# Two expert stages re-ordered into 36 block-and-chunk steps, with chunk-wise sums in PSUM and the weight products moved inside

## The chip, the cores and the metric
The program runs on one core of a Trainium2 chip. A core has a matrix engine (TensorE, PE in the profile, with PEld for its weight loads), a vector engine (VectorE, DVE), a scalar engine (ScalarE, ACT), GpSimd (POOL) and SyncE (SP), which here issues nearly all DMA transfers. Each engine has its own list of instructions and waits for the others by semaphores. The metric is the device time of one execution in microseconds (us), lower is better.

## The reference
A two-layer network in float32 on tokens `x` of 4 x 512 with 128 features. Each half layer normalises the tokens and adds its result to them. The order that the kernel follows is: an expert stage (half weight), linear attention, a second expert stage (half weight, the same weights), then the second layer's product-key feed-forward part and softmax attention, and the feed-forward part once more.

The expert stage matters here. Per token, 16 gate scores pass through a sigmoid; the two best of four groups and the four best experts in them are chosen, and their weights are normalised:

```
scores = sigmoid(x @ w_gate.T)
...
w = w / (w.sum(-1) + 1e-6)
out = sum_e w[e] * (silu(x @ w1[e].T) * (x @ w3[e].T)) @ w2[e].T  +  shared expert
```

Linear attention, which follows, uses random features: `phi(t) = relu(t @ RF)` for queries and keys, `kv = phi_k^T v`, and `out = phi_q kv / (phi_q sum(phi_k)) @ W_out`. Since RF and W_out act on fixed weights, products of weights with weights (W_qk with RF, W_v with W_out, and W_q with the keys of the feed-forward part) can be formed before any token is needed.

## The kernel before
**The stages.** `net` (L1505) runs `moe` (first expert stage), `linear_fold` and `peer_fold` (products of weights), `linear_attn`, `moe` again, `peer_and_scores`, `attn` and `peer`.

**An expert stage.** The 2,048 tokens are four blocks of 512. All 16 experts of 64 hidden features lie side by side as eight chunks of 128 columns; the shared expert of 128 is a ninth chunk, index `NCH` = 8, which needs no gate weight. `hidden` (L335) makes one chunk for a block of tokens: two matrix products of 128x512 (`pg` L342, `pu` L344), a silu on ACT (L346) and a product on DVE (L350, or L348 for the ninth chunk). `weigh` (L353) multiplies a chunk by the spread gate weights on POOL (L355). `out` (L357) makes the result of 128 tokens: nine accumulated products in one PSUM tile `po` (L360), and DVE adds half of it to the tokens (`residual`, L175). So `out` of the first 128 tokens needs all nine weighted chunks of the block.

**The gate.** `stats` and `normed` normalise a block (DVE, with two small POOL operations L111 and L113), `scores` (L227) turns it on PE (L230), copies it on ACT (L232), and makes the gate logits (L238) and the sigmoid (L242). Then come four pieces on DVE, the chain: `pairs` (L244, seven operations), `groups` (L277, nine), `best` (L289) and `choose` (L304), whose last operation writes the weights `w` (L318). `weights` (L332) turns `w` on PE (`pcT` L324), copies it on ACT (`cT` L326), writes it to memory with one DMA (L165), and reads it back with two DMAs of 1 MB (L170), spread over the partitions.

**The order.** Inside `moe` the order of PE, DVE, ACT and POOL is that of the Python program (`manual_schedule`, L202). The first block makes its nine chunks while the gates of blocks 0 and 1 are worked out; all of its multiplications on POOL stand behind it (L420). From the second block on, the outputs of the block before are made between the last four chunks (L408), each chunk is weighed one step later (L417), and the last block's outputs stand at the end (L425). Products `pg` and `pu` take turns in five PSUM tiles (`m_ps`, L199). Outside `moe` a scheduler orders the instructions.

**Other work in the first expert stage.** Behind block 0 stands `distances` (L992: small operations on DVE and ACT, and 22 small DMAs), behind block 1 the loads for linear attention (`linear_loads`, four DMAs, 2.25 MB), behind block 2 the loads for the second layer (`peer_weights` and `attn_weights`, 22 DMAs on SP). Loads are issued by SP in this order, between the DMAs of the gate weights. `linear_fold` (L441) and `peer_fold` (L630) are then 112 passes of PE over 64 rows each, all passes of one half of the rows before those of the other half, each group copied out by ACT or DVE. At the start, the token loads alternate between SP's and ACT's queues (L80).

Of the kernel before, what the change touches and what calls it, by code (L numbers as in the profile page):

```python
# [10 lines left out]
FP = mybir.dt.float32  # L11
AF = mybir.ActivationFunctionType
# [5 lines left out]
P = 128  # L18
# [44 lines left out]
class Net:  # L63
# [12 lines left out]
    def tokens(self, lo, hi):  # L76
        x_tok = self.t["x"].flatten_outer_dims()
        for i in range(lo, hi):
            xi = self.const.tile([P, DIM], FP, tag=f"x{i}", name=f"x{i}")
            eng = self.nc.sync if i % 2 else self.nc.scalar  # L80
            eng.dma_start(xi, x_tok[i * P : (i + 1) * P, :])
            self.xs.append(xi)
# [110 lines left out]
    def moe(self, behind=None, ahead=None):  # L193

        nc, tc = self.nc, self.tc
        with (
# [123 lines left out]
            def given(w):  # L320

                pc = ps1.tile([NE, SEQ], FP, tag="gate", name="pcT")
                for i in range(BT):
                    nc.tensor.transpose(pc[:, i * P : (i + 1) * P], w[:, i, :], self.ident)  # L324
                cT = sb.tile([NE, SEQ], FP, tag="cT", name="cT")
                nc.scalar.copy(cT, pc)  # L326
                return self.spread(sb, sd, [(cT, slice(0, NE))])

            class Experts(Gate):


                def weights(u):  # L332
                    u.cw = given(u.w)

                def hidden(u, *cs):  # L335
                    if not hasattr(u, "hT"):
                        u.hT = sb.tile([P, NCH + 1, SEQ], FP, tag="hT", name="hT")
                        u.hs = {}
                    for c in cs:
                        cols = slice(c * P, (c + 1) * P)  # L340
                        pg = ps.tile([P, SEQ], FP, tag="mm", name="pg")
                        nc.tensor.matmul(pg, self.w1[:, cols], u.xT, start=True, stop=True)  # L342
                        pu = ps.tile([P, SEQ], FP, tag="mm", name="pu")
                        nc.tensor.matmul(pu, self.w3[:, cols], u.xT, start=True, stop=True)  # L344
                        g = sb.tile([P, SEQ], FP, tag="g", name="g", bufs=NCH + 1)
                        nc.scalar.activation(g, pg, AF.Silu)  # L346
                        if c == NCH:
                            nc.vector.tensor_tensor(u.hT[:, c, :], pu, g, ALU.mult)  # L348
                        else:
                            nc.vector.tensor_tensor(g, pu, g, ALU.mult)  # L350
                            u.hs[c] = g

                def weigh(u, *cs):  # L353
                    for c in cs:
                        nc.gpsimd.tensor_tensor(u.hT[:, c, :], u.hs[c], u.cw[:, c, :], ALU.mult)  # L355

                def out(u, i):  # L357
                    po = pso.tile([P, DIM], FP, tag="po", name="po")
                    for c in range(NCH + 1):
                        nc.tensor.matmul(  # L360
                            po,
                            u.hT[:, c, i * P : (i + 1) * P],
                            self.w2[:, c, :],
                            start=(c == 0),
                            stop=(c == NCH),
                        )
                    self.residual(u.blk * BT + i, po, 0.5)

            def chain(u):
                return [u.pairs, u.groups, u.best, u.choose]

            behind = behind or {}
            blocks = [Experts(blk) for blk in range(NB)]
            if ahead:
# [8 lines left out]
            for blk in range(NB):  # L385
                now, last = blocks[blk], blocks[blk - 1] if blk else None
                after = blocks[blk + 1] if blk + 1 < NB else None
                parts = []
                now.hidden(NCH)
                if last is None:  # L390
                    parts = chain(now)
                elif after:
                    after.scores()
                    parts = chain(after)
                for c in range(NCH):
                    if parts:
                        parts.pop(0)()
                    now.hidden(c)
                    if last is None:
                        if c == 3:  # L400
                            after.scores()
                            parts = chain(after)
                        if c == 4:
                            now.weights()
                        if c in (5, 6):
                            blocks[c - 3].stats()
                    else:
                        if c >= NCH - BT:  # L408
                            last.out(c - NCH + BT)
                        if after and c == 4:  # L410
                            after.weights()
                        if ahead and (blk, c) in ahead:
                            ahead[blk, c](ps)
                    if c == 7 and blk + 2 < NB:
                        blocks[blk + 2].normed()
                    if last and c:
                        now.weigh(c - 1)  # L417
                if last is None:
                    after.weights()
                    now.weigh(*range(NCH))  # L420
                else:
                    now.weigh(NCH - 1)
                for f in behind.get(blk, []):
                    f()
            for i in range(BT):  # L425
                now.out(i)
# [14 lines left out]
    def linear_fold(self, pool):  # L441


        nc, tc = self.nc, self.tc
        self.wf = wf = pool.tile([P, 2, H * DH], FP, tag="wf", name="wf")
        self.wvo = wvo = pool.tile([P, NHP, 2, DIM], FP, tag="wvo", name="wvo")
        self.bout = self.load(pool, "bout", [P, DIM], self.t["b_out"].partition_broadcast(P))
        self.tiny = pool.tile([P, 1], FP, tag="tiny", name="tiny")
        nc.vector.memset(self.tiny, 1e-6)
        with tc.tile_pool(name="af_ps", bufs=4, space=PSUM, reuse_waits="tile") as ps:  # L450
            for s in range(2):
                for odd in range(2):
                    r = slice(odd * DH, (odd + 1) * DH)
                    pf = ps.tile([P, NHP, DH], FP, tag="pf", name="pf")
                    for k in range(NHP):
                        nc.tensor.matmul(
                            pf[:, k, :],
                            self.wqkT[r, s * NHP + k, :],
                            self.rf[r, k, :],
                            start=True,  # L460
                            stop=True,
                        )
# [1163 lines left out]
```

## Time and profile before

| what | us | from |
|---|---|---|
| median of three runs | 1448.12 | times |
| lowest and highest | 1443.87, 1449.14 | times |
| profiled execution, first to last instruction | 1447.6 | the page |
| first expert stage, to the last `po` | 0 to 130.6 | timeline of PE |
| products of weights | 130.6 to 149.4 | timeline of PE |
| linear attention | 149.4 to 310.1 | timeline of PE |
| second expert stage | 310.1 to 426.8 | timeline of PE |
| the rest | 426.8 to 1447.6 | timeline of PE |

Of the profiled execution only the span is given; its own device time is not listed apart from the three runs, whose median lies 0.5 us above the span. In the two expert stages PE was busy 111.1 of 130.6 us and 106.6 of 116.7 us, POOL 49.2 and 45.1 us. A row of the timeline gives the start, the length of a run of equal instructions, the engine, the line, and in brackets how long the engine sat idle before and what ended that. One matrix product in float32 is two passes of PE, so `x2` is one product of 512 columns; at full clock such products follow each other every 0.86 us, though one is listed with 1.02 us because its end overlaps the next. Lengths near 1.9 us for the same thing are passes at half clock.

### The profile page before, as it was taken

How to read it: one execution, taken by the hardware profiler on the slowest of the kernel's cores; microseconds unless marked ns; L12 is line 12 of the kernel's file. 1: busy time of each engine (PE TensorE's matmuls, PEld its weight loads, DVE VectorE, ACT ScalarE, POOL GpSimd, SP SyncE). 2: the span in 40 equal slices, each digit the busy share in tenths (PEclk: the TensorE clock that was granted, in tenths of full speed). 3: DMA queues.
4: the chain of work that ended last, by engine and by line, in shares of the span. 5: the costliest groups of instructions: out<-in, count | busy, mean ns of one | idle time of the engine just before them, and what ended most of it. 6: DMA issues, size and time to landing. Idle time of an engine off the chain costs nothing.

```text
span 1447.6 us, 32427 instructions
## 1 busy us (share of the span) xinstructions
PE 1211.2 (84%) x12424; PEld 772.2 (53%) x12424; DVE 917.5 (63%) x2583; ACT 846.0 (58%) x1621; POOL 754.3 (52%) x760
## 2 busy tenths in 40 slices
PE   6899989987995789798887589899899889777776
PEld 3559566654662555555564145465464555544455
DVE  5642422257529887977953166666676677598997
ACT  4331323332227577676644488978778778487774
POOL 1532333215347978888967014435344443478874
PEclk9898899998997799999988789999999999988888
DMA  3583041215500035343449878978889874000000
GB/s 107 112 195 112 1 103 42 59 35 130 106 1 1 29 103 189 117 163 142 175 183 285 305 214 233 278 204 244 256 223 274 234 208 126 8 2 6 6 8 10
DMA packets 180805, 189.23 MB, mean 131 GB/s; under 512 B 44091, under 2 KB 155307, under 8 KB 180523
## 3 DMA queue, kind: packets, MB, share of 16 engines
q1 hardware_dynamic: 177930, 185.51, 44.5%
q8 instruction: 98, 1.61, 0.5%
q10 hardware_dynamic: 2592, 1.64, 0.4%
q14 instruction: 57, 0.46, 0.1%
q0 software_dynamic: 128, 0.01, 0.0%
HBM read 135.13 MB, written 52.13 MB: 129 GB/s over the span
## 4 chain that ended last, share of the span: by engine, by line
PE 44%; DVE 19%; ACT 16%; POOL 8%; DMA 6%; issue 4%; SPq 1%; ACTq 0%; DVEq 0%; POOLq 0%
ACT F L1325 6%; DVE wt L822 5%; PE po L360 4%; PE pg L342 4%; PE pu L344 4%; PE pq L1128 4%; DVE rep L783 3%; ACT ht L1290 3%; PE po L1409 3%; PE p L1088 3%; PE ph L1277 3%; POOL al L758 2%; DMA F<-S 2%; PE pk L503 2%; PE pu L525 2%
## 5 line engine op out<-in xcount | busy, mean ns | idle before, releaser
L1265 POOL TENSOR_TENSOR F<-F,kz 128x512 f32<-128x512 f32 (+10 forms) x88 | 164.5, 1872 | 263.4 <-DMA F<-S 183.4
L758 POOL TENSOR_TENSOR al<-sim 128x512 f32<-128x512 f32 x128 | 138.6, 1114 | 42.9 <-ACT sim L717 39.4
L1310 DVE CUSTOM_DVE_ANT_0 F<-pf,F 128x64 f32<-128x64 f32 (+21 forms) x256 | 99.4, 437 | 84.3 <-PE pf L1299 42.6
L1290 ACT ACTIVATE ht<-ph,b 128x2048 f32<-128x2048 f32 (+7 forms) x65 | 102.2, 1572 | 84.6 <-PE ph L1277 84.5
L1325 ACT ACTIVATE F<-F,mn 128x64 f32<-128x64 f32 (+21 forms) x256 | 129.7, 508 | 0.3
L1142 ACT ACTIVATE st<-pq 128x256 f32<-128x256 f32 (+3 forms) x128 | 82.8, 698 | 71.1 <-PE pq L1128 37.8
L355 POOL TENSOR_TENSOR hT<-g,spread 128x512 f32<-128x512 f32 x64 | 79.7, 1268 | 79.0 <-DVE g L350 51.5
L1128 PE MATMUL pq<-k,q 32*128 32x256 f32 (+3 forms) x1024 | 102.5, 493 | 12.0 <-POOL q L1105 9.0
L828 POOL TENSOR_TENSOR wt<-wt 128x1152 f32<-128x1152 f32 x32 | 84.1, 2627 | 48.7 <-DVE wt L822 44.7
L1356 DVE COPY wT<-pt 128x512 f32<-128x512 f32 (+1 forms) x176 | 104.4, 635 | 7.0 <-PE pt L1350 4.8
L815 ACT ACTIVATE wt<-al,z 128x576 f32<-128x576 f32 x128 | 88.8, 768 | 29.4 <-DVE z L808 20.0
L346 ACT ACTIVATE g<-pg 128x512 f32<-128x512 f32 x72 | 42.7, 597 | 103.3 <-PE pg L342 96.6
L783 DVE MATCH_REPLACE8 rep<-top,al 128x576 f32<-128x576 f32 x128 | 95.1, 743 | 0.0
L1299 PE MATMUL pf<-ht,w2b 64*32 64x512 f32 (+16 forms) x1408 | 86.8, 538 | 8.2 <-ACT ht L1290 8.2
L1350 PE MATMUL pt<-ident,F 128*128 128x128 f32 x640 | 91.1, 285 | 0.5 <-issue 0.5
L884 PE MATMUL po<-up,cT 128*128 128x128 f32 x256 | 45.5, 332 | 53.8 <-DVE cT L880 53.8
L822 DVE SCALAR_TENSOR_TENSOR wt<-rep,wt 128x2304 f32<-128x2304 f32 x32 | 88.5, 2764 | 0.0
L1409 PEld LDWEIGHTS po<-wT,v 128*64 128x64 f32 x2560 | 76.9, 138 | 20.3 <-DVE wT L1356 9.4
L1350 PEld LDWEIGHTS pt<-ident,F 128*128 128x128 f32 x640 | 72.3, 145 | 27.8 <-issue 14.7
L1409 PE MATMUL po<-wT,v 128*64 128x64 f32 x2560 | 80.6, 223 | 4.0 <-DVE wT L1356 2.1
L1098 DVE TENSOR_TENSOR t<-p,cos 128x512 f32<-128x512 f32 x64 | 43.8, 685 | 59.4 <-POOL k L1106 28.1
L344 PE MATMUL pu<-ln_xT,w 128*128 128x512 f32 x144 | 78.3, 627 | 2.6 <-DVE g L350 2.6
(218 smaller groups left out, 2833.3 us busy)
## 6 DMA issues: line engine op xcount, KB each, us to landing
spread<-rows SPq DMA_DIRECT2D x24, 1024.0 KB
S<-st SPq DMA_DIRECT2D x32, 512.0 KB
S<-st SPq DMA_DIRECT2D x32, 384.0 KB
V<-v SPq DMA_DIRECT2D x16, 512.0 KB
S<-st SPq DMA_DIRECT2D x32, 256.0 KB
v<-V SPq DMA_DIRECT2D x16, 512.0 KB
F<-S SPq DMA_DIRECT2D x24, 256.0 KB
S<-st SPq DMA_DIRECT2D x32, 128.0 KB
```

The lines of the kernel that those rows point to most:

```text
L344: nc.tensor.matmul(pu, self.w3[:, cols], u.xT, start=True, stop=True)
L758: nc.gpsimd.tensor_tensor(u.al[:, h, :NEAR].rearrange("p (i j) -> p i j", j=NK), bc(u.sim[:, 0, h, :TK], 2, NK), bc(u.sim[:, 1, h], 1, TK) ...
L783: nc.vector.match_replace(u.rep[:, h, :], u.top[:, h, :], u.al[:, h, :ALL], LOWEST)
L822: nc.vector.scalar_tensor_tensor(wf, u.rep.rearrange("p h k -> p (h k)"), TAKEN, wf, ALU.is_lt, ALU.mult)
L1128: nc.tensor.matmul(pq[hh // 2][:, hh % 2, :J], u.q[r, t, a, :], u.k[r, t, a, :J], start=(a == 0), stop=(a == 1), tile_position=(hh * 32, 0),)
L1265: nc.gpsimd.tensor_tensor(u.F[:, :, :J], u.F[:, :, :J], win, ALU.add)
L1290: nc.scalar.activation(ht, x, AF.Gelu, bias=self.b1)
L1310: nc.vector.tensor_tensor_reduce(F, pf[k % 2][:, k // 2, :J], F, -1.0, -LOWEST, ALU.add, ALU.min, mn[:, g : g + 1],)
L1325: nc.scalar.activation(F, F, AF.Exp, bias=mn[:, g : g + 1], scale=-1.0, accum_out=sm[:, g : g + 1],)
L1350: nc.tensor.transpose(pt[:, at : at + P], u.F[:, m - 1 - s0 - s, j * P : (j + 1) * P], self.ident,)
L1356: nc.vector.tensor_copy(u.unit.wT[:, js.start : js.stop, :, q : q + w * GQ].rearrange("p j h (r q) -> p j h r q", q=2), pt[:, : len(js) * ...
L1409: nc.tensor.matmul(po[o * DH : (o + 1) * DH, c, :], vs[u.t.n - u.t.ib + j][:, h * DH : (h + 1) * DH], u.wT[:, j, h, x : x + nq], start=(j ...
```

## The change
A stage becomes one row of 36 steps, a step being a block and a chunk, the ninth chunk of each block first. In step k, `hidden` makes chunk k. From step 10 on, up to two chunks are weighed per step, at most up to chunk k-2, and up to two chunks go into the output. `out` now adds one chunk to all four token tiles of the block, in one PSUM tile of 128x4x128, and only the last chunk's turn is followed by four `residual`s. The weighted chunks `hT` are single tiles, five in all; the unweighted ones, `g`, have fourteen. The gates of the later blocks are worked out at fixed steps. The spread weights come back in eight DMAs of 256 KB per block instead of two of 1 MB.

In the first stage the other work becomes hooks at fixed steps: the loads for linear attention at step 17, `distances` at 20, the loads of the second layer at 22, and the products of weights at steps 29 to 32 and 35, with the two halves of the rows alternating. `linear_fold` and `peer_fold` as stages of their own are gone. An activation table that serves both exp and ln is loaded once in `distances`. All token loads but the first four go through SP's queue.

```diff
-            eng = self.nc.sync if i % 2 else self.nc.scalar
+            eng = self.nc.sync if i % 2 or i >= BT else self.nc.scalar
...
+                    for c in range(0, NCH, 2):
+                        w = sb.tile([P, 2, SEQ], FP, tag="spread", name="spread", bufs=NCH)
+                        for o in range(2):
+                            at = d[2 * c + o : 2 * c + 4 : 2, :]
+                            at = bass.AP(at.tensor, at.offset, [[0, DH], *at.ap])
+                            nc.sync.dma_start(w[o * DH : (o + 1) * DH], at)
+                        u.cw += [w[:, 0, :], w[:, 1, :]]
...
+                def weigh(u, c):
+                    if c < NCH:
+                        h = sb.tile([P, SEQ], FP, tag="hT", name="hT", bufs=5)
+                        nc.gpsimd.tensor_tensor(h, u.hs[c], u.cw[c], ALU.mult)
+                        u.hs[c] = h
+
+                def out(u, c):
+                    first, last = c == NCH, c == NCH - 1
+                    if first:
+                        u.po = pso.tile([P, BT, DIM], FP, tag="po", name="po")
+                    for i in range(BT):
                         nc.tensor.matmul(
+                            u.po[:, i, :],
+                            u.hs[c][:, i * P : (i + 1) * P],
                             self.w2[:, c, :],
+                            start=first and not i,
+                            stop=last and i == BT - 1,
+                        )
+                    if last:
+                        for i in range(BT):
+                            self.residual(u.blk * BT + i, u.po[:, i, :], 0.5)
...
+            chain(0, blocks[0])
+            at(4, blocks[0].weights)
+            at(5, blocks[1].scores, blocks[2].stats)
+            chain(6, blocks[1])
+            at(7, blocks[2].normed)
+            at(11, blocks[1].weights)
+            for blk in (1, 2):
+                k, u = blk * SL, blocks[blk + 1]
+                at(k + 3, u.scores)
+                chain(k + 4, u)
+                at(k + 8, u.weights)
+            at(SL + 6, blocks[3].stats)
+            at(SL + 8, blocks[3].normed)
+            chunks = [(u, c) for u in blocks for c in (NCH, *range(NCH))]
+            weighed, done = 0, 0
+            wait, lag = 10, 2
+            for k in range(len(chunks) + 8):
+                if k < len(chunks):
+                    u, c = chunks[k]
+                    u.hidden(c)
+                for f in hooks.get(k, ()):
+                    f(ps)
+                for f in todo.pop(k, ()):
                     f()
+                ahead = weighed
+                if k >= wait:
+                    n = 0
+                    while n < 2 and weighed < len(chunks) and weighed <= k - lag:
+                        u, c = chunks[weighed]
+                        u.weigh(c)
...
+                while n < 2 and done < ahead - 1 + (k >= len(chunks)):
+                    u, c = chunks[done]
+                    u.out(c)
...
+    def fold_features(self, s, ps):
+        pf = [ps.tile([P, NHP, DH], FP, tag="mm", name="pf") for _ in range(2)]
+        for k in range(NHP):
+            for odd in range(2):
+                r = slice(odd * DH, (odd + 1) * DH)
+                nc.tensor.matmul(
+                    pf[odd][:, k, :],
+                    self.wqkT[r, s * NHP + k, :],
+                    self.rf[r, k, :],
...
+        for odd in range(2):
+            self.evac(odd, dst[:, :, odd, :], pf[odd])
...
+        nc.scalar.preload_act_table_set("natural_log_exp_and_others")
         nc.scalar.activation(ab, ab, AF.Exp)
...
             n.moe(
                 {
-                    0: [lambda: n.distances(aw, ks, kd, nd)],
-                    1: [lambda: pinned((n.linear_loads, lw))],
-                    2: [lambda: pinned((n.peer_weights, pw, mw), (n.attn_weights, aw, qw))],
+                    17: [lambda ps: pinned((n.linear_loads, lw))],
+                    20: [lambda ps: n.distances(aw, ks, kd, nd)],
+                    22: [lambda ps: pinned((n.peer_weights, pw, mw), (n.attn_weights, aw, qw))],
+                    29: [lambda ps: n.fold_features(0, ps)],
+                    30: [lambda ps: n.fold_features(1, ps)],
+                    31: [lambda ps: n.fold_values(0, ps)],
+                    32: [lambda ps: n.fold_values(1, ps)],
+                    35: [lambda ps: n.fold_keys(ps)],
                 }
             )
-            n.linear_fold(mw)
-        n.peer_fold()
+            n.bout = n.load(mw, "bout", [P, DIM], t["b_out"].partition_broadcast(P))
+        nc.gpsimd.tensor_scalar(n.bd, n.bd, 0.5, None, ALU.mult)
         n.linear_attn(qw)
```

`fold_values` and `fold_keys` have the same form as `fold_features`, for W_v with W_out and for W_q with the keys.

## The prediction
> **What bounds the kernel now.** I read the page first, then the chain of waits: up to 430 us it is nearly all PE (`po`, `pg`, `pu`, `pf`, `pk`). So a microsecond that PE idles or runs at half clock in these stages is a microsecond of the total. The timeline of PE, before the change, then shows where that happens:
>
> ```profile
> 38.39 0.60 PE L324 MATMUL pcT<-ident,w 128*16 128x128 f32 x4 [4.35 <-DVE w L318]
> 46.70 1.89 PE L238 MATMUL pl<-wg,ln_xT 128*128 128x16 f32 x8 [3.86 <-ACT ln_xT L232]
> 48.43 2.05 PE L342 MATMUL pg<-ln_xT,w 128*128 128x512 f32 x2
> ...
> 120.46 10.21 PE L360 MATMUL po<-w,hT 128*128 128x128 f32 x90
> 130.60 2.00 PE L456 MATMUL pf<-rf,wqkT 64*128 64x64 f32 x16
> 149.40 1.45 PE L128 MATMUL ln_pt<-ident,xn 128*128 128x128 f32 x4 [0.87 <-DVE xn L125]
> ...
> 333.66 1.01 PE L324 MATMUL pcT<-ident,w 128*16 128x128 f32 x4 [4.34 <-DVE w L318]
> 349.38 1.96 PE L344 MATMUL pu<-ln_xT,w 128*128 128x512 f32 x2 [2.60 <-DVE g L350]
> ```
>
> PE waits for the gate chain on DVE, runs at half clock after each such wait (1.9 to 2.05 for a product of 1.02), and spends 130.6 to 149.4 on the products of weights alone. Why DVE is late is in its own timeline against POOL's:
>
> ```profile
> 322.04 0.22 DVE L318 TENSOR_TENSOR w<-w,ws 128x64 f32<-128x64 f32 x1
> 341.13 1.30 DVE L249 TENSOR_TENSOR hi<-s 128x32 f32<-128x32 f32 x1 [2.24 <-ACT s L242]
> 342.35 1.30 DVE L250 TENSOR_TENSOR lo<-s 128x32 f32<-128x32 f32 x1
> 372.00 0.18 DVE L250 TENSOR_TENSOR lo<-s 128x32 f32<-128x32 f32 x1
> ```
>
> ```profile
> 338.67 9.82 POOL L355 TENSOR_TENSOR hT<-g,spread 128x512 f32<-128x512 f32 x8 [4.73 <-DMA spread<-rows]
> ```
>
> The same operation takes 0.18 us with POOL idle and 1.30, the length of one POOL multiplication, while POOL multiplies back to back. Products out of PSUM (L350, 0.69) don't suffer. The old order kept most chains clear of POOL; the new one does not.
>
> **The change part by part.** Dense PE work of a stage is unchanged: 36 steps of 1.72 (`pg`+`pu`) and 0.89 (a quarter of the four 9-product outputs, 8.03 per block), gates 2.04 each, `pcT` 0.44. I count what is lost beside it.
>
> Start: ACT's first table load waits until 9.21 because six token loads hold its queue for 6.38 us (2.80 to 9.18); `ln_pt` on PE is done at 7.85. With those loads on SP the copy ends at 8.4 instead of 11.1: -2.7 (nothing at the least, if `w1` lands later). SP issues six more loads ahead of `w2` and `tri`, about 0.5 each; `tri` is wanted at 17.5, some 4 us after issue: nothing.
>
> Losses of before, removed: idle 4.35+3.86 and 4.34+2.60+1.13; half clock after them, from the distance of starts against 0.86 a product, 4.5 in the first stage and 4.2 in the second. Sum -25.0.
>
> Losses of after, by following the new order with the same durations:
> (a) `weights` of block 0 stands after five steps instead of six and a gate. Second stage: step 4 ends at 310.9+5x1.72=319.5, `w` is there at 322.2: 2.7. First stage: 22.7 against 21.6: 1.1. Together 3.8.
> (b) Gate chain of block 1, the largest term. PE could pass step 11 in the second stage at 322.3+0.44+1.72+2.04+6x1.72=336.9. The chain starts after `g` of step 6, 329.7; alone it takes pairs 0.9, groups 2.0, `normed` 1.1, best 1.2, choose 1.1 and the products between, 9.0 in all: 338.7, a wait of 1.8. But the spread weights land piecewise: rows issued 323.4, first read 1.6 later, then (2 MB took 12.26 from issue, some 2 of it latency) the first pair 4.6 later: POOL starts at 329.6, runs ahead of its place in the program and makes five multiplications (five `hT` tiles, the first freed by an output after step 12) to 336. Rows give 0.65 us per affected operation (seven in 4.5 at 49.8 to 54.2) to 1.05 (seven in 7.4 at 341.1 to 348.6), against 0.13. Pairs then end at 334.2, `w` at 342.2: 5.3; at 1.05 it is 6.7. While DVE is late, `g` stands behind the chain, so PSUM tiles stay full and `hidden` waits too; it is the same wait, not another. Bounds 1.8 and 6.7; I take 5.3, worked out from the lower row. The first stage has the same distances: 10.6.
> (c) Block 2's chain, steps 13 to 16: POOL busy 2.5 of 3.5 us a step, and four statistics (1.6) and four residuals (0.85) stand before choose. 0 if unhindered, 2.3 at 1.05: 1.5 per stage, 3.0.
> (d) Block 3's chain, steps 22 to 25, 2.61 a step, POOL busy half of it: own time 8.0 of 9.8 available, plus 2.4 in place of 1.1 for `normed` of the next stage (that row under POOL, L652, x4: 2.46): 0 to 2.2 in the second, 0 to 0.9 in the first; 1.5 together.
> (e) `distances` at step 20: ACT's Exp and two Ln wait for DVE, behind them on ACT are silu of step 21 and the copy of block 3's gate, for which PE waits, as it did before (3.86). One table load of 1.28 goes. 4.1 (3.8 to 5.5).
> (f) Block 3's row and eight reads stand on SP behind 22 DMAs of `distances` and 22 loads (4.2 MB). Before, the same two groups took 48.0 to 71.0 and 96.1 to 122.5, both with a spread in their midst (12 and 8 us). From step 20 (88 us) that makes the row's issue about 118 to 125 and its first pair 124 to 131; PE wants it at step 32, about 126. 0 to 6, taken 2. What waits is POOL, then PE's output queue. The loads of step 17 go out behind block 1's reads and are done before block 2's: nothing. The 48 additional read issues (0.63 each) fall where SP is idle.
> (g) Half clock after waits of 2.6 to 5 us: 1.75 to 2.6 each in the rows; three such waits at 1.7: 5.1 (1.7 to 8.7).
> Sum of a to g: +30.1.
>
> Products of weights: 18.8 exposed go. 112 passes as filler cost 0.12 each (first 16 before: 1.93 us) if the alternating halves gain nothing, 0.06 if two run at once; the row for row tiles (512-column passes of `pq` L1128, 16 in 3.52, against 0.43 for a full-height one) speaks for some gain. 6.7 to 13.4, taken 9. They were also the cover of linear attention's first normalisation: it needs only old tokens, but DVE has it behind block 3's residuals. Residuals 0.9, four statistics 1.1, POOL 0.23+1.04, `xn` 0.34 and hand-overs: 4.5 idle for PE (0.9 at the least), where 0.87 showed. -18.8+9+4.5=-5.3.
>
> Sum: -2.7-25.0+30.1-5.3=-2.9. Against the profiled span of 1447.6 that is 1444.7; the median lies 0.5 above the span: **1445**. 0.5% (7.2 us) is about what a measurement can tell here, so this is a small gain lost in it.
>
> The Trainium skill's page "SBUF — State Buffer", section "Who interferes with whom", says why the chain suffers: a vector instruction with two SBUF inputs, or in a two-port mode, shares GpSimd's read path, and the one that comes second is blocked for the other's whole instruction. The trace agrees (0.18 against 1.30). By the rule alone, one 1.25 us block for each of fifteen operations in (b), the term would be bounded by POOL's 6.4 us of work, so 6.7 and a sum of -0.1. The page "TensorE: Matmul & The Clock Gate", section "What's actually happening", puts re-throttling at an idle window of about 3.4 us; here 2.60 idle was followed by slow passes (349.38), and the row decides.
>
> **The rivals.**
> *Clear of each other.* POOL's multiplications miss the chains (later landing, or DVE gets more operations between): b 1.8 per stage, c and d 0 but for 0.5, f 0, g one wait of 1.7, fill 6.7. -7.0-3.0-1.0-2.0-3.4-2.3=-18.7: **1426**. For it: chains at 372 and 77 ran at full speed beside a little POOL work. Against it: POOL is now at work in every step.
> *POOL always in the way (slower).* Place: chains of blocks 1 to 3 in both stages. At 1.05 per operation without pauses: b 6.7 (+2.8), c 5 per stage (+7), d 4 (+2.5), one or two more half-clock stretches (+3): +15.3, **1460**. It decides from about 0.8 per operation in all three chains. For it: eight multiplications in a row at 338.67. Against: five `hT` tiles make POOL pause whenever PE does.
> *Late weights of block 3.* f 6 to 9 alone: **1450**. For it: the order of SP's queue; against: pairs land singly, and outputs of block 2 and fillers come first.
>
> **How the numbers follow.** Forecast 0.40 (own range 1436 to 1455), clear 0.30, in the way 0.22, late weights 0.08. Faster than 1440.9: 0.11 of the forecast's and 0.29 of the first rival's; slower than 1455.4: 0.02, 0.18 and 0.03; the rest within. The range leaves out the ends of the two outer rivals, 0.1 each: 1425 to 1460.
>
> **What would show it.** Right: `w` L318's successor waits at `pcT` of block 1 of some 5 us in both stages, DVE operations of the chain at 0.6 to 1.3 us, the first `pg` near 10 us instead of 12.9, first `ln_pt` of linear attention at about 146 after some 4 us idle, second stage as long as before (116 to 118 us). Wrong: a second stage of under 110 us (the chain is not hindered) or over 124 (it is hindered throughout); `hT` on POOL waiting for `spread` near 125 us for more than 3 us (f); fold passes far from 9 us; later stages, which are unchanged, moved by more than 3 us.

## The result and the profile after

The changed kernel takes 1453.03 us (median) where the kernel before takes 1449.21 beside it: a ratio of 1.0031, 95% interval 1.0018 to 1.0044. It is 0.2 to 0.4% slower. That is less than the 0.5% that the prediction took as what a measurement can tell, but the interval does not contain 1, so the loss is clear of the scatter. The forecast was 1445, with a gain of 2.9 us in its sum; the time lies inside the range, the sign is wrong.

| start of, in us from the span's start | before | after |
|---|---|---|
| first `pg` of the first expert stage | 12.87 | 10.24 |
| linear attention (its first `ln_pt`) | 149.40 | 146.15 |
| first `psim`, right behind the second expert stage | 426.84 | 435.62 |
| end of the span | 1447.6 | 1450.1 |

Up to the linear attention the change gains 3.25 us. Between there and `psim` it loses 12.0: the second expert stage costs 10.7 more than before, the linear attention 1.3. The last rows seem to say that the unchanged stages behind got 6.3 us shorter; further profiles settle that below (they did not).

The timeline of PE in the changed kernel, with its waits (start, length, line, product, and in brackets the idle time before and what ended it):

```profile
10.24 2.06 PE L347 MATMUL pg<-ln_xT,w 128*128 128x512 f32 x2
...
21.91 0.60 PE L330 MATMUL pcT<-ident,w 128*16 128x128 f32 x4 [1.20 <-DVE w L321]
...
42.16 1.01 PE L330 MATMUL pcT<-ident,w 128*16 128x128 f32 x4 [5.37 <-DVE w L321]
42.97 1.91 PE L367 MATMUL po<-w,g 128*128 128x128 f32 x8
...
67.18 1.20 PE L367 MATMUL po<-w,hT 128*128 128x128 f32 x8 [1.89 <-POOL hT L358]
68.17 1.91 PE L347 MATMUL pg<-ln_xT,w 128*128 128x512 f32 x2
...
88.09 1.40 PE L241 MATMUL pl<-wg,ln_xT 128*128 128x16 f32 x8 [3.23 <-ACT ln_xT L235]
...
146.15 1.45 PE L128 MATMUL ln_pt<-ident,xn 128*128 128x128 f32 x4 [4.14 <-DVE xn L125]
148.28 9.71 PE L539 MATMUL pk<-wf,ln_xT 128*128 128x512 f32 x16 [0.68 <-ACT ln_xT L130]
...
320.47 0.77 PE L330 MATMUL pcT<-ident,w 128*16 128x128 f32 x4 [2.68 <-DVE w L321]
...
342.32 1.01 PE L330 MATMUL pcT<-ident,w 128*16 128x128 f32 x4 [3.67 <-DVE w L321]
...
367.39 1.16 PE L367 MATMUL po<-w,hT 128*128 128x128 f32 x8 [1.89 <-POOL hT L358]
...
404.23 1.01 PE L330 MATMUL pcT<-ident,w 128*16 128x128 f32 x4 [4.23 <-DVE w L321]
```

The waits of before (4.35, 3.86, 4.34, 2.60) are gone, and others stand in their places: every block's `weights` step now has PE waiting at `pcT` for `w`, or at an output for `hT`. Behind most of these waits a product takes 1.9 us in place of 1.02 (or 1.05 for `po`), that is, half clock; the profile's windows view gives a granted clock of 0.50 from 342 to 348 us, behind the wait of 3.67. The row at 21.91 shows the exception: behind 1.20 us of waiting the four transposes take 0.60, where they take 1.01 at 42.16.

Why `w` is late can be read from DVE's and POOL's timelines of the changed kernel, side by side. First the gate chain of block 1 on DVE:

```profile
31.89 0.77 DVE L268 TENSOR_TENSOR eq<-gs 128x64 f32<-128x64 f32 x1
32.69 1.21 DVE L269 TENSOR_TENSOR eq<-eq,tri 128x64 f32<-128x64 f32 x1
...
35.18 1.21 DVE L275 TENSOR_TENSOR gt<-gt,eq 128x64 f32<-128x64 f32 x1
...
36.88 0.22 DVE L288 TENSOR_TENSOR mk<-s,rk 128x64 f32<-128x64 f32 x1
```

Then POOL in the same kernel:

```profile
30.05 6.25 POOL L358 TENSOR_TENSOR hT<-g,spread 128x512 f32<-128x512 f32 x5 [1.99 <-DMA spread<-rows]
...
64.55 0.23 POOL L111 TENSOR_SCALAR ln_ve<-ln_mv 128x4 f32<-128x4 f32 x1 [8.30 <-DVE ln_mv L109]
...
65.87 9.97 POOL L358 TENSOR_TENSOR hT<-g,spread 128x512 f32<-128x512 f32 x8
```

From 30.05 to 36.3 POOL makes five multiplications, and in that time operations of the chain with two inputs in SBUF (the on-chip memory that both engines read) take 0.77 to 1.32 us (the longest, at 33.83, lies between the rows shown); the same kind takes 0.22 at 36.88. At 64.55 something else shows that the prediction had not named: POOL stands 8.3 us at the statistics of block 3's norm, which the program has ahead of block 1's multiplications, and these then come eight in a row.

### The profile page after: what moved, and what is told of

It is laid out like the page before. It is cut to its first block, busy times and chain, and to the rows that moved or that the text cites. A ratio compares the mean times of both kernels' runs of the same rounds, so it can differ in the third digit from the quotient of the medians.

```text
span 1450.1 us, 32526 instructions
## 1 busy us (share of the span) xinstructions
PE 1199.5 (83%) x12424; PEld 758.0 (52%) x12424; DVE 928.0 (64%) x2582; ACT 843.8 (58%) x1620; POOL 755.4 (52%) x760
## 3 DMA queue, kind: packets, MB, share of 16 engines
q10 hardware_dynamic: 1728, 1.25, 0.3%
## 4 chain that ended last, share of the span: by engine, by line
PE 38%; DVE 23%; ACT 17%; POOL 10%; DMA 6%; issue 4%; SPq 1%; ACTq 0%; POOLq 0%; DVEq 0%
ACT F L1347 6%; DVE wt L843 5%; ACT ht L1312 4%; PE po L367 4%; DVE rep L804 4%; PE pg L347 3%; PE ph L1299 3%; PE pq L1150 3%; PE pu L349 3%; PE po L1431 3%; POOL al L779 3%; PE pk L539 2%; PE pu L561 2%; DMA F<-S 2%; PE pq L549 2%
## 5 line engine op out<-in xcount | busy, mean ns | idle before, releaser
L352 DVE TENSOR_TENSOR g<-pu,g 128x512 f32<-128x512 f32 x72 | 49.4, 688 | 94.4 <-PE pu L349 85.7
L347 PE MATMUL pg<-ln_xT,w 128*128 128x512 f32 x144 | 80.6, 644 | 0.0
```

## The experiments

The theories:

- **A, lock.** POOL's multiplications stretch the gate chains of blocks 1 to 3, and PE waits for `w`.
- **B, steps.** The `weights` steps stand too early, whatever POOL does.
- **C, bound.** POOL is the limit behind the chains: what starts later on it ends later, and PE waits for `hT` in place of `pcT`.
- **D, queue.** The waits of 1.89 us come from the place of block 3's statistics in POOL's queue.
- **E, clock.** The half clock behind each wait is a cost of its own, about 15 us in all.

The times and ratios here are against the kernel before, run beside each variant; "`psim`" is the start of the first `psim` in the variant's profile (426.84 before, 435.62 after).

| kernel | median us | ratio (95%) | `psim` |
|---|---|---|---|
| the change | 1453.03 | 1.0031 (1.0018 to 1.0044) | 435.62 |
| e_small_weigh | 1425.83 | 0.9851 (0.9837 to 0.9865) | 407.70 |
| e_later | 1433.41 | 0.9902 (0.9889 to 0.9916) | 411.85 |
| e_stats3 | 1449.36 | 1.0006 (0.9993 to 1.0018) | 422.71 |
| e_second_old | 1444.05 | 0.9973 (0.9957 to 0.9988) | 425.79 |
| e_warm | 1446.63 | 0.9988 (0.9972 to 1.0005) | 424.29 |
| e_both | 1429.15 | 0.9853 (0.983 to 0.9876) | 401.07 |
| e_dist | 1426.68 | 0.985 (0.9832 to 0.9868) | 402.58 |
| e_wait12 | 1426.59 | 0.9847 (0.9828 to 0.9866) | 401.49 |
| e_start | 1446.48 | 0.9986 (0.9973 to 0.9998) | 425.13 |
| e_fold_apart | 1457.31 | 1.006 (1.0039 to 1.0081) | 436.86 |
| e_lead | 1412.22 | 0.9757 (0.9733 to 0.978) | 391.41 |

### POOL's multiplications made short

```diff
-                        h = sb.tile([P, SEQ], FP, tag="hT", name="hT", bufs=5)
-                        nc.gpsimd.tensor_tensor(h, u.hs[c], u.cw[c], ALU.mult)
-                        u.hs[c] = h
+                        h = u.hs[c]
+                        nc.gpsimd.tensor_tensor(h[:, :8], h[:, :8], u.cw[c][:, :8], ALU.mult)
```

> The changed kernel with GpSimd multiplying only 8 of the 512 columns of each expert chunk (the weights of the other 504 are left out of the result); every step stays where it is. Theory A, GpSimd's multiplications hold the vector engine's routing chain up: the waits at pcT of blocks 1 and 3 (5.37, 5.0, 1.44, 4.23) fall below 2 each, the two waits of 1.89 at the outputs go, and with them most of the half clock behind them (about 10 of 15 us); in all 1421 to 1432 us. The pcT waits of block 0 (1.20 and 2.68), where GpSimd does not multiply yet, stay. Theory B, the steps of weights() are simply too early for the chain, whatever GpSimd does: the pcT waits stay near their size, only the 1.89s go, 1444 to 1449 us.

1425.83 us, `psim` 27.9 us sooner: theory A's number. The same operations on DVE in this run:

```profile
32.16 0.21 DVE L268 TENSOR_TENSOR eq<-gs 128x64 f32<-128x64 f32 x1
32.41 0.23 DVE L269 TENSOR_TENSOR eq<-eq,tri 128x64 f32<-128x64 f32 x1
...
32.80 0.23 DVE L275 TENSOR_TENSOR gt<-gt,eq 128x64 f32<-128x64 f32 x1
```

And PE in this run, at block 1 of the first stage and at blocks 0 and 1 of the second:

```profile
38.81 0.60 PE L330 MATMUL pcT<-ident,w 128*16 128x128 f32 x4 [0.73 <-DVE w L321]
...
309.59 0.91 PE L330 MATMUL pcT<-ident,w 128*16 128x128 f32 x4 [2.68 <-DVE w L321]
...
326.90 0.60 PE L330 MATMUL pcT<-ident,w 128*16 128x128 f32 x4 [0.73 <-DVE w L321]
```

The three operations shown in both fall from 3.19 us to 0.67. Block 1's wait falls from 5.37 and 3.67 to 0.73, blocks 2 and 3 have none at `pcT` any more, and 0.83 is left at each output that waited 1.89. Block 0's waits, where POOL does not multiply yet, stay at 1.19 and 2.68. So A holds for the waits at `pcT` of blocks 1 and 3, and B for block 0 alone; the outputs of 1.89 are taken up under D. What remains of "too early" in block 1 is 0.73 us.

### The weights steps later

```diff
-            at(4, blocks[0].weights)
+            at(5, blocks[0].weights)
-            at(11, blocks[1].weights)
+            at(13, blocks[1].weights)
-                at(k + 8, u.weights)
+                at(k + 9, u.weights)
```

> The changed kernel with weights() of block 0 one step later (step 5), of block 1 two (13), of blocks 2 and 3 one (k + 9), so that TensorE has hidden chunks to do while the chain ends. Theory A (the waits at pcT and the half clock behind each are the price): one step is 1.72 us of hidden chunk and, from block 1 on, 2.6 with its output; so 3.9 + 10.4 + about 4 of the 5.7 go, and some 10 of the 15 us of half clock; less what later weights cost: 1430 to 1440 us. Theory C (GpSimd is the bound behind it: what starts later ends later, and TensorE waits for hT in place of pcT): new waits of TensorE for GpSimd of 3 to 6 us per stage, 1446 to 1455 us.

1433.41 us. Block 1's chain is as slow as before (12.8 us from its first operation at 28.52 to `w`, 12.6 in the changed kernel), but PE has hidden chunks to do while it ends. Against C: POOL does not become the bound. Some of what is left on PE's timeline in this run:

```profile
38.53 1.12 PE L347 MATMUL pg<-ln_xT,w 128*128 128x512 f32 x2 [1.69 <-DVE g L352]
...
60.09 1.16 PE L367 MATMUL po<-w,hT 128*128 128x128 f32 x8 [1.89 <-POOL hT L358]
61.08 1.02 PE L347 MATMUL pg<-ln_xT,w 128*128 128x512 f32 x2
...
348.83 1.95 PE L367 MATMUL po<-w,hT 128*128 128x128 f32 x8 [1.90 <-POOL hT L358]
```

`po` at 348.83 takes 1.95, half clock; the one at 60.09 takes 1.16. Part of the chain's delay has moved to `pg`, which waits 1.69 us for a free tile because `g` stands behind the chain on DVE: the lock is hidden, not gone. The two waits for `hT` are still there, as theory D says, since this edit doesn't touch POOL's order.

### Block 3's statistics sooner

```diff
-            at(7, blocks[2].normed)
+            at(7, blocks[2].normed, blocks[3].stats)
-            at(SL + 6, blocks[3].stats)
```

> The changed kernel with the statistics of block 3's norm at step 7 in place of step 15, so that GpSimd does not stand 8.3 us behind a reciprocal square root ahead of block 1's multiplications. Theory D (that place in GpSimd's queue makes the waits of 1.89 us at the outputs in both stages): both waits go, 3.8 us and 2 to 4 us of half clock: 1445 to 1448 us, less if the chain of block 1 is the longer for the statistics (up to 2 us a stage). Against it (GpSimd is behind anyway): the waits stay, 1451 to 1455 us.

The waits of 1.89 us are gone in both stages, so D is right about their cause. In their place PE waits 0.97 and 0.96 us at block 2's `pcT` for `w`, which the longer waits had hidden. The time lies between the two expectations. In the profile `psim` starts 12.9 us sooner than in the changed kernel; the median, 1449.36, gives 3.6 us by the ratios. The profiled execution is the fastest of this kernel's, 5.0 us below its median, so part of the 12.9 is that execution; where the other executions are longer isn't known. The direction is the same in both.

Why more than 3.8 us went in that profile begins in POOL's timeline of this run:

```profile
35.50 0.23 POOL L111 TENSOR_SCALAR ln_ve<-ln_mv 128x4 f32<-128x4 f32 x1 [7.58 <-DVE ln_mv L109]
...
36.81 6.20 POOL L358 TENSOR_TENSOR hT<-g,spread 128x512 f32<-128x512 f32 x5
```

At step 7 the statistics hold POOL too, but now ahead of its first multiplication, which begins at 36.81 in place of 30.05 and so misses most of block 1's chain. But the four statistics now stand in that chain, so block 1's waits fall only from 5.37 to 4.10 and from 5.00 to 4.11. All the waits together are 4.3 us shorter. The larger part of the 12.9 is half clock: worked out from the starts behind each wait, it is 6.3 us behind four waits, where the changed kernel has 15.0 behind seven.

### Both, and the first multiplication later

> The later weights() and the statistics of block 3 at step 7, together. What is left of waits in the run with later weights alone is 1.69 us (the hidden chunk, for the vector engine) and two of 1.89 and 1.90 (outputs, for GpSimd), 0.96 and 1.61 at pcT. If the two edits add up, the 1.89s go with their half clock (about 5 us in the two stages): 1427 to 1430 us against 1433.4. If the statistics only lengthen block 1's chain, which in the run with them alone still ended 4.1 us late, the gain turns into a longer wait at the hidden chunk or pcT: 1431 to 1436.

1429.15 us; in the profile no wait of block 1 or 2 is left in either stage, beyond the 0.7 us at each gate. The edits add up. Then, in addition, POOL's first multiplication two steps later:

```diff
-            wait, lag = 10, 2
+            wait, lag = 12, 2
```

> The two edits together, and GpSimd's first multiplication at step 12 in place of 10, so that block 1's routing chain (steps 6 to 9) ends before GpSimd multiplies. Theory A (multiplications hold the chain): block 1's chain ends 4 to 5 us sooner, the wait of 1.7 us at the hidden chunk in both stages goes with 1 to 2 us of half clock: 3 to 6 us below the run without. Against it: outputs begin two steps later and catch up two a step until step 24, in which GpSimd (1.29 us a chunk, 2.57 for two, against 2.61 a step) is the bound, and waits of TensorE for hT come in its place: 0 to 5 us above.

1426.59 us and a ratio of 0.9847 against 0.9853 for the run without it: no difference, and neither expectation met. The wait that this edit was to remove had already gone: POOL's first multiplication starts at 36.11 here and at 35.38 without, held there by the statistics in both.

### Half clock by itself

```diff
+        FILL = {False: (0, 6, 0, 0), True: (3, 4, 0, 5)}
                     pc = ps1.tile([NE, SEQ], FP, tag="gate", name="pcT")
+                    for _ in range(FILL[ready][u.blk]):
+                        nc.tensor.matmul(pc, self.w1[:, :NE], u.xT, start=True, stop=True)
```

> The changed kernel with needless products ahead of pcT, written into pcT's own tile and then overwritten, that fill the four long waits but for some 0.2 us: six of 0.86 us in the first stage's block 1, three, four and five in the second stage's blocks 0, 1 and 3. No wait of the program goes. Theory E (the half clock behind a wait is a cost by itself): behind the four waits the passes run at 0.43 us at once, 2.7 + 1.7 + 2.8 + 2.6 us less: 1441 to 1445 us against 1453. Against it (what TensorE gains there it waits again at the next tile of the vector engine or GpSimd, or the clock falls whatever is done): 1450 to 1456 us.

More work, and it is faster: 0.9988 (0.9972 to 1.0005) against 1.0031 (1.0018 to 1.0044), some 6 us, with `psim` 11.3 us sooner in the profile (9.8 expected up to there). The median of 1446.63 misses the expected 1441 to 1445 by 1.6. PE around block 1's `pcT` in this run:

```profile
36.96 5.32 PE L331 MATMUL pcT<-ln_xT,w 128*16 128x512 f32 x12
42.27 0.60 PE L333 MATMUL pcT<-ident,w 128*16 128x128 f32 x4
42.72 1.06 PE L370 MATMUL po<-w,g 128*128 128x128 f32 x8
43.61 1.02 PE L350 MATMUL pg<-ln_xT,w 128*128 128x512 f32 x2
```

`pcT`'s transposes start at 42.27, no sooner than the 42.16 of the changed kernel, but the products behind them take 1.06 and 1.02 in place of 1.91 and 1.91. The windows view says it in one number, the granted clock (the number behind POOL's busy time and count) from 310 to 350 us. The changed kernel:

```profile
310.00:350.00 40.00, 30.97 (x88) 15.02 (x87) 25.52 (x99) 14.74 (x23) 8.80 (x9) 0.87 0.30 72
```

The same with the waits filled:

```profile
310.00:350.00 40.00, 37.08 (x138) 18.27 (x137) 27.10 (x102) 15.79 (x24) 11.37 (x10) 1.00 0.44 100
```

The second stage takes 118.9 us here in place of 127.5, and those 8.6 us are nearly the 8.9 of half clock that the changed kernel has in this stage. So E is shown: beside its length, a wait can cost 1.7 to 2.8 us of half clock behind it. The price is not fixed. The wait of 1.89 at 360.21, which this edit leaves in place, is followed by full speed here, and the one of 3.23 at 85.53 by a loss of 3.4 us, twice what the changed kernel has there.

### One part alone: the first stage, the start, the products of weights

For the first, the second expert stage is called by the old function; everything else is as changed.

> The changed kernel with the second expert stage as in the kernel before, the first stage, the fold and the start as changed: one part alone. By the two traces the first part alone gains 3.25 us up to the norm of the linear attention, the linear attention loses 1.3, and the second stage is 116.7 us again in place of 127.5. If the 6.3 us by which the stages after it were shorter in the changed kernel's trace are scatter of single executions, 1445 to 1448 us; if they belong to the changed second stage, 1447 and its later stages as long as before; if they belong to the changed start or first stage, 1440 to 1442.

1444.05 us, just under the 1445 expected, and 0.27% below the kernel before (0.12 to 0.43%): the start, the first stage and the products of weights together gain some 4 us, and the new second stage alone turns this into a loss. The unchanged stages behind took 1021.5 us here, so they were not shortened by the changed start or first stage.

The start by itself, as an edit of the kernel before:

```diff
-            eng = self.nc.sync if i % 2 else self.nc.scalar
+            eng = self.nc.sync if i % 2 or i >= BT else self.nc.scalar
```

> The kernel before, with only the token loads as changed (blocks 1 to 3 on SyncE's queue alone). If the start's gain reaches the end, as the first row of the traces says (10.24 against 12.87 us): 1444 to 1446 us beside 1447.5 to 1449. If the wait for SyncE's queue is paid back at a later load: within 1 us of the kernel before.

Ratio 0.9986 (0.9973 to 0.9998), 2.0 us: most of the gain of the first row (10.42 against 12.87 in the kernel before) reaches the end.

The products of weights behind the last output, halves still alternating:

```diff
-                    29: [lambda ps: n.fold_features(0, ps)],
...
-                    35: [lambda ps: n.fold_keys(ps)],
+            with tc.tile_pool(name="af_ps", bufs=4, space=PSUM, reuse_waits="tile") as ps:
+                n.fold_features(0, ps)
...
+                n.fold_keys(ps)
```

> The changed kernel with the products of weights by weights taken out of block 3 and put behind the last output, with their halves alternating as changed and four tiles. Theory F (alternating the halves is the gain, not the place: 7.1 us of passes against 18.8): the last output ends 7 us sooner, the products take 7 to 9 us where TensorE waits 4.1 us for the norm now, and the norm follows them: the linear attention begins within 2 us of the changed kernel's 146.2, 1451 to 1455 us. Theory G (the place is the gain: apart, they run on half clock behind the copies of four tiles as before): 8 to 12 us later, 1460 to 1465 us.

PE in this run:

```profile
123.38 1.56 PE L367 MATMUL po<-w,hT 128*128 128x128 f32 x8 [4.23 <-POOL hT L358]
...
137.55 3.79 PE L469 MATMUL pf<-rf,wqkT 64*128 64x64 f32 x64
...
147.59 1.45 PE L128 MATMUL ln_pt<-ident,xn 128*128 128x128 f32 x4 [3.38 <-DVE xn L125]
```

And POOL in this run:

```profile
122.06 6.25 POOL L358 TENSOR_TENSOR hT<-g,spread 128x512 f32<-128x512 f32 x5 [16.64 <-DMA spread<-rows]
```

Theory F is right about the passes: from 137.55 to about 144.2 they take some 6.7 us apart, where the kernel before took 18.8: at first 0.12 a pass at a granted clock of 1.00 (131 to 134 us), then 0.21 at 0.50 (136 to 149 us). Here it is 0.06 a pass at 1.00. So the alternating order is the gain, not the place. The linear attention begins 1.4 us later than with them as filler. The median, 1457.31, lies above F's 1451 to 1455, although its interval overlaps that of the change. But the place has a worth that F left out: without the filler PE reaches block 3's first output sooner and waits 4.23 us for POOL, and POOL for the weights' reads behind the loads on SP. That is the wait that the prediction's term (f) looked for; the filler hides it.

### The distances later, and the norm of the linear attention sooner

```diff
-                    20: [lambda ps: n.distances(aw, ks, kd, nd)],
+                    24: [lambda ps: n.distances(aw, ks, kd, nd)],
```

> The two edits together, and the distances of the later attention issued at step 24 in place of 20, so that ScalarE's table loads do not stand ahead of block 3's ln_xT (the wait of 3.24 us at pl in every trace of the changed first stage). If the five tiles between TensorE and ScalarE take up the 4 us of distances where no copy waits behind them, 3 us and 1 of half clock go: 3 to 4 us below the run without. If ScalarE's time is simply missing there, a wait of the same size comes at a hidden chunk: the same within 1.5 us.

0.985 against 0.9853 without: nothing gained. The wait of 3.23 us at `pl` is gone, and this one stands in its place, on PE's timeline of this run:

```profile
90.79 2.08 PE L367 MATMUL po<-w,hT 128*128 128x128 f32 x8 [4.04 <-POOL hT L358]
```

It is not at a hidden chunk, as the expectation had it, but at an output: POOL stands 9.37 us at the `memset` of `distances`, until DVE is done with that tile, and 5.00 us of multiplications stand behind it. This is the queue effect of theory D once more.

The last run keeps `distances` where it was, has the three edits of e_wait12, and takes the first block's norm out of the linear attention (its tokens are finished since block 1):

```diff
+                    25: [lambda ps: n.lead_stats(mw)],
+                    28: [lambda ps: n.lead_normed(mw)],
+                    33: [lambda ps: n.lead_turned(mw, ps, "mm")],
...
-                xn = sb.tile([P, BT, DIM + 1], FP, tag="xn", name="xn")
-                nc.gpsimd.memset(xn[:, :, DIM], 1.0)
-                xT = self.norm_T(b, sb, ps, "mm", xn)
+                if b:
+                    xn = sb.tile([P, BT, DIM + 1], FP, tag="xn", name="xn")
+                    nc.gpsimd.memset(xn[:, :, DIM], 1.0)
+                    xT = self.norm_T(b, sb, ps, "mm", xn)
+                else:
+                    xn, xT = self.lead_xn, self.lead_xT
```

`lead_stats`, `lead_normed` and `lead_turned` do for the linear attention what `first_stats`, `first_normed` and `first_turned` do for the stage behind the second expert stage.

> Later weights, block 3's statistics at step 7, the first multiplication at step 12, and the norm of the linear attention's first block during block 3 (statistics at step 25, normalized at 28, turned at 33, as the second stage already does for its successor), so that TensorE goes on to the keys without the wait of 4.05 us for the norm and 0.68 for the copy. If the wait and the half clock behind it (the keys' first row took 10.21 us) are the price: 6 to 8 us below the 1426.6 of the run without, 1418 to 1421 us. If the vector engine and GpSimd are short of time in block 3, or the linear attention waits for its second block's norm instead: 1424 to 1428 us.

1412.22 us, 2.4% below the kernel before (2.2 to 2.7%), more than expected. In the profile 10.1 us of the gain over e_wait12 lie ahead of `psim`; the rest of the 14 by the medians is not located. PE at the seam of the two stages:

```profile
124.02 4.73 PE L367 MATMUL po<-w,hT 128*128 128x128 f32 x40
128.59 7.03 PE L541 MATMUL pk<-wf,lead_xT 128*128 128x512 f32 x16
```

No wait, and the keys take 7.03 us in place of 9.71 in the changed kernel and 8.83 in the kernel before. This version beats both.

### Is the part behind the change really shorter?

> The changed kernel once more, unaltered, for a second profile. In the first one the stages up to the later attention's first product of keys ended 8.8 us later than before (435.62 against 426.84), and the stages behind it, which the change does not touch, took 1014.5 us against 1020.8. Scatter of single executions: the waits up to 435.6 come again within 1 us, the rest takes 1017 to 1023 us, as in the profiles of the other variants. A gain behind the change that hides its loss: 1013 to 1016 us again.

> The kernel before once more, unaltered, for a second profile of it. Its first one reached the product after the second expert stage at 426.84 us and took 1020.8 behind it; the medians give the change 4 to 6 us, the two profiles of the changed kernel (435.62 and 435.85) 9. If a kernel's stages up to there repeat as the changed kernel's did, within 1 us, the 9 us stand, and the difference to the medians lies in the unaltered stages behind. If they come out at 429 to 432, the first profile of before was a lucky one and the loss up to there is 4 to 6.

> The same once more, as a third profile: 426 to 428 us up to the second expert stage's end if it repeats, and 1014 to 1024 behind it.

> The changed kernel a third time: 435 to 437 us up to the second expert stage's end, and behind it 1014 to 1024 if that part scatters alike in both kernels; 1014 to 1018 if it is shorter behind the change.

| profile | `psim` | from there to the end |
|---|---|---|
| before | 426.84, 426.02, 428.26 | 1020.8, 1020.9, 1018.3 |
| after | 435.62, 435.85, 434.64 | 1014.5, 1020.9, 1020.8 |

In the same order as the expectations (the first profile, `after_again` or `before_again`, the third). Up to `psim` each kernel repeats within 2.3 us, and the loss is 8.3 (435.37 less 427.04, the means). The 1014.5 did not come again: it was one execution's scatter. `after_again` also repeats the timing of the change, 1454.24 and 1.0032 (1.0015 to 1.0049). The intervals of the medians reach to about 7 us, somewhat less than the 8.3 of the profiles; what the rest is stays open, within a part that varies from 1014.5 to 1023.9 over all the profiles.

## Why the prediction was wrong

| step | predicted | measured |
|---|---|---|
| start | -2.7 | -2.63 (alone -2.0, by the medians) |
| losses of before removed | -25.0 | -25.0 (the same rows) |
| (a) weights of block 0 | 3.8 | 1.20 + 2.68 = 3.88 |
| (b) block 1's chain under POOL | 10.6 | 5.37 + 1.33 + 3.67 = 10.37 |
| (c) block 2's chain | 3.0 | 1.89 + 1.89 = 3.78, by another cause |
| (d) block 3's chain | 1.5 | 1.44 + 4.23 = 5.67 |
| (e) distances | 4.1 | 3.23 |
| (f) reads behind loads | 2 | 0 |
| (g) half clock | 5.1 | 15.0 |
| products of weights, norm wait | -18.8+9+4.5 | -18.8+7.1+4.1 |
| linear attention longer | not counted | 1.3 |
| sum | -2.9 | +8.0 |

The sum of the measured terms, 8.0, stands beside the 8.8 of the profile's `psim`; the medians show about half of that, as said above. (g) is worked out as the prediction did it, from the distance of starts behind each wait: 2.7, 1.8 and 1.7 in the first stage, 1.7, 2.8, 1.8 and 2.55 in the second.

**The step that failed is (g).** It charged three waits with the lowest price in the rows of before (they give 1.7, 2.9, 2.5 and 1.8), 1.7 each. Seven waits were followed by half clock, at 2.1 on average, 15.0 us, and the bound of 8.7 was passed too. The price was too low, and so was the number. By the prediction's own terms four waits were of 2.6 us or more: 2.7 in (a), 5.3 twice in (b) and 4.1 in (e). The other three were two of 1.89, below the lengths that it priced (2.6 to 5), and the 4.23 that (d) had too small. e_warm shows this kind of loss by itself, with 8.6 us of it in the second stage. The term is 9.9 of the 10.9 by which the sum missed; the other misses, of both signs, nearly cancel. The second stage took 127.5 us, more than the 124 that the prediction had named as a sign against it.

**(d) failed too, by 4.2**, nearly all of it in the second stage (4.23 against a bound of 2.2). Its own time for the chain, 8.0 us, was right: with POOL nearly still the chain takes 8.1 (e_small_weigh) and this wait is gone. In the changed kernel it takes 12.8, since POOL stretches two operations of `pairs` (0.93 and 1.32), one of `groups` (1.29), the `xn` of the next stage's norm (2.11 in place of 1.11) and one of `choose` (1.00 in place of 0.17). The prediction named only the `xn` as stretched and put the chain's end almost inside the 9.8 us that it had.

**(c) had the right size by luck, and the wrong cause.** It was put down to the chain; the waits are for `hT`, because the statistics of block 3 hold POOL's queue. The prediction had followed the queues of SP and ACT, but had not looked on POOL's for an instruction that itself waits. e_stats3 removes these waits without touching block 2's chain, which then costs 0.97 and 0.96.

**(b) was right** in mechanism and size, including the five multiplications ahead of their place. Its lower bound of 1.8 was too high: alone, the chain costs 0.73 (e_small_weigh).

**(f) could be nothing, as the prediction allowed**: the waits are hidden, and e_fold_apart shows what it costs without the cover, 4.23. So "late weights of block 3" is no cause here, though its 1450 lies near the result.

**The products of weights** came out close to the lower bound: halves in pairs, 0.06 a pass. The row that the prediction leaned on spoke for more than it read there: 512-column passes of `pq` are listed with 2.00 to 2.90 us for 16 in all rows but one (3.47), and none with 3.52. That the norm would then show (4.5, seen 4.14) was right. Left out was that more half clock follows it: the keys' products take 9.71 us in place of 8.83. The other 0.4 of the linear attention's 1.3 is not located.

**The rivals.** "Clear of each other" is refuted by block 1's rows. "POOL always in the way" had the sign and was nearer on block 3 (4 against 5.67), but it charged 10 us to the chains of block 2, for whose `w` PE did not wait in the changed kernel. The missing price is mostly half clock.

The Trainium skill's page "SBUF — State Buffer", section "Who interferes with whom", said that vector operations with two SBUF inputs are blocked until the GpSimd instruction ends; 0.77 to 1.32 us against 0.22, beside multiplications of 1.25, agrees. The page "TensorE: Matmul & The Clock Gate", section "What's actually happening", names an idle window of about 3.4 us; the runs had half clock behind waits of 1.89, and the measurement decides.

## What to carry to other kernels

Price a wait of TensorE as its length plus the half clock that may follow it, and count every wait of about 2 us, not only the long ones: here this added 15.0 us to 26.9 us of waits. Where the engine that feeds a wait can't be made faster, put dense work in front of the waiting instruction: moving the `weights` steps by one or two chunks was worth 1.3% (0.9902 against 1.0031). After each reordering, read every engine's queue for an instruction that waits on another engine with urgent work behind it: a short statistics instruction and a `memset` on POOL, each waiting for DVE, held 10 us (in the changed kernel) and 5 us (in e_dist) of multiplications.

## What the runs showed of the hardware that was not expected

- Needless products on TensorE made the kernel faster (0.9988 against 1.0031), since the clock granted between 310 and 350 us rose from 0.87 to 1.00.
- A wait's length alone does not decide whether the clock falls. Waits of 1.20 (at 21.91 in the changed kernel) and 1.69 (e_later, 38.53) were followed by full speed; 1.89 was followed by half clock at 67.18 in the changed kernel and by full speed at 60.09 in e_later and at 360.21 in e_warm; 2.68 by half clock at 320.47 in the changed kernel. In e_stats3 the same wait of 2.68 was followed by full speed, as its PE timeline has it:

```profile
315.62 0.60 PE L330 MATMUL pcT<-ident,w 128*16 128x128 f32 x4 [2.68 <-DVE w L321]
316.06 1.02 PE L347 MATMUL pg<-ln_xT,w 128*128 128x512 f32 x2
```

What decides beside the length stays open; no run here tested it.
